# Set-up work of a fused four-layer kernel placed in other steps: bias scaling, decay, layer norm, w2 products and the adaptive layer

## The chip, the cores and the metric

The kernel runs on one core of a Trainium2 chip. A core has a matrix engine (TensorE, "PE" in the profile), a vector engine (VectorE, "DVE"), an activation engine (ScalarE, "ACT"), a general engine (GpSimd, "POOL") and an engine that only issues transfers (SyncE, "SP"). Each works through its own list of instructions in order and waits on semaphores for the others. Transfers are issued from SP, ACT or POOL. The metric is the time of the launch on the device in microseconds (us), the median of several runs.

## The reference

The input x has shape (4, 1024, 512): 4 sequences, 1024 time steps, width 512. Beside it there is one condition vector per sequence, cond (4, 512). Four layers are applied, each added to its own input:

```
x = x + rnn(x, h0=cond)           # h_t = tanh(x_t Wx0 + b0 + h_{t-1} Wh0)
x = x + ssm(x, conv_w=cond)       # conv of 4 taps, softplus, scan s_t = decay*s_{t-1} + dt*b_t*u_t, Wo
x = x + lstm(x, h0=cond)          # gates from x_t Wx2 + b2 + h_{t-1} Wh2
x = x + (x @ layer)               # layer = base + einsum(x_a, x_b), per sequence
    ae = layernorm(cond) * ln_g + ln_b
    x_a, x_b = split(gelu(ae @ w1 + b1) @ w2 + b2)    # w2 is (512, 2*512*8): 16.8 MB in float32
```

Two things are serial in time: the RNN and the LSTM, 1024 steps each. What depends on cond and weights alone (decay, folded convolution weights, the pieces of Wh2, the matrices `layer`) is worked out once.

## The kernel before, in words

Time is cut into 32 chunks of `TC` = 32 steps. `do_pass(c)` is one pass of 32 steps: in each step it does one LSTM step of chunk c, one RNN step of chunk c + 2, and spreads over the steps the projections for the RNN of chunk c + 3, the SSM layer of chunk c + 1, the LSTM's input products of chunk c + 1, and the adaptive layer of chunk c - 1. There are two passes ahead: pass -2 runs the RNN of chunk 0 alone, pass -1 the RNN of chunk 1 and the SSM of chunk 0. Pass 0 is the first with an LSTM.

Nothing is scheduled by a planner: the order on each engine is the order in which the Python code emits it (`manual_schedule`). Within step t of a pass this is: LSTM matmuls (L360), the jobs of place "pe" for this t, RNN matmuls (L335), the LSTM's vector and activation work with the jobs of place "gap", the RNN's transpose, add and tanh (L343, L344, L347), then what the dictionary `early` holds for (c, t), then the jobs of place "end". `early` carries the set-up work; `at(c, t, f)` adds to it.

The pieces of set-up that matter here, with their places before:

- `prepare_decay` (L243): 17 small VectorE instructions and one Exp, emitted ahead of pass -2.
- `scale_b2` (L263), step (-2, 0): scales the LSTM's bias. b2 arrives by 16 small transfers on the POOL queue.
- `split_wh2`, steps (-2, 4) to (-2, 29): cuts the 16 pieces of Wh2 in the tile `layer` into three bfloat16 parts each, on ScalarE and VectorE.
- `fold_conv` (L250), step (-2, 30): folds cond into the convolution weights.
- `load_late`, step (-2, 30): issues w1, the first four tiles of w2 and base on SP; they go to the parts of `layer` that the splitting has freed.
- `adapt_norm` and `adapt_hidden`, step (-1, 0): layer norm of cond, two sums over the width by matmuls with a matrix of 1/512 (L529, L540), Sqrt, then the product with w1 (L561) and Gelu.
- `adapt_w2(j)`, j = 0 to 31: one product of the hidden vector with a tile of w2 (16 matmuls of 64 columns, L578), four copies out of PSUM (L583), and the load of tile j + 4. The first 16 stand in every other step of pass -1, the other 16 in steps 0 to 15 of pass 0. After each half, `adapt_gather` moves the pieces by 16 small transfers on POOL.
- `adapt_bias`, `adapt_sum` (0, 19), `base_identity` (0, 0): transposes of b2's part, sums, and twice the identity added to base (16 VectorE instructions, L626).
- `adapt_layer(b, k)`, 16 of them, steps (0, 20) to (0, 31), four of these steps with two: a matmul of depth 8 over 512 columns (L617) and an addition that writes `layer` (L618).

All small results pass through two PSUM banks of tag "fill".

## Time and profile before

| | us |
|---|---|
| median of 3 runs | 4838.51 (4836.14 to 4839.81) |
| the profiled execution | 4832.98 |
| its span, first to last instruction | 4831.2 |
| first RNN matmul / second / third | 21.38 / 24.97 / 40.45 |
| first RNN matmul of pass -1 | 123.31 |
| first LSTM matmul of pass 0 / of pass 1 | 207.60 / 386.71 |

| engine | busy us | share of the span |
|---|---|---|
| TensorE | 4612.2 | 95% |
| VectorE | 3830.2 | 79% |
| ScalarE | 1734.0 | 36% |
| GpSimd | 50.2 | 1% |

The page shows one profiled execution. "L335" is a line of the code. In a timeline each line gives the start in us, the length, the engine, the line, the operation, output and input tiles with shapes, and in brackets how long the engine sat idle before it and what released it. A table by stretch gives for each stretch its length, the busy time of PE, PEld (TensorE's weight loads), DVE, ACT and POOL with the number of instructions, the clock that TensorE was granted (1.00 is full speed), the share of the DMA engines' time, and GB/s.

### The profile page before, as it was taken

The page shows a single profiled execution, that of the slowest core. Times are in us where ns is not written, and L with a number is a line of the kernel's source. Part 1 is how long each engine was busy: PE and PEld are TensorE (multiplying, and loading weights), DVE is VectorE, ACT ScalarE, POOL GpSimd, SP SyncE. Part 2 cuts the span into 40 slices and gives each one's busy share as a digit, 9 for nine tenths or more (in the row PEclk, how much of TensorE's full clock was granted, in tenths as well). Part 3 has the DMA queues.
Part 4 walks back from the last instruction along what each step waited for, and adds up shares of the span by engine and source line. Part 5 has one row for each costly group of instructions (what it writes and reads, how often), then busy time and mean ns, then how long its engine had stood idle before and what let it go on. Part 6 is the DMA issues. An engine that isn't in the chain of part 4 may idle for free.

```text
span 4831.2 us, 321596 instructions
## 1 busy us (share of the span) xinstructions
PE 4612.2 (95%) x147040; PEld 3528.0 (73%) x147040; DVE 3830.2 (79%) x17908; ACT 1734.0 (36%) x8647; POOL 50.2 (1%) x94
## 2 busy tenths in 40 slices
PE   5899999999999999999999999999999999999876
PEld 3677777777777777777777777777777777777654
DVE  3588887888888888888888888888888888888776
ACT  2233333333333333333333333333333333333332
POOL 2000000000000000000000000000000000000000
PEclk6999999999999999999999999999999999999999
DMA  6310000000000000000000000000000000000000
GB/s 135 100 35 9 9 9 7 7 9 9 9 9 7 9 7 9 9 9 9 7 7 9 9 9 9 7 9 7 9 9 9 7 9 7 9 7 7 6 3 7
DMA packets 38786, 67.46 MB, mean 14 GB/s; under 512 B 9056, under 2 KB 26080, under 8 KB 36400
## 3 DMA queue, kind: packets, MB, share of 16 engines
q1 hardware_dynamic: 33488, 45.63, 3.6%
q8 instruction: 1149, 18.83, 1.6%
q10 hardware_dynamic: 1728, 1.06, 0.1%
q14 instruction: 213, 1.74, 0.1%
q0 software_dynamic: 2208, 0.19, 0.1%
HBM read 38.34 MB, written 8.39 MB: 10 GB/s over the span
## 4 chain that ended last, share of the span: by engine, by line
PE 93%; DVE 5%; DMA 1%; issue 1%; ACT 0%; POOL 0%; DVEq 0%; SPq 0%; POOLq 0%
PE acc L360 58%; PE acc L335 18%; PE proj L316 9%; PE pb L290 3%; PE proj L290 2%; PE ada L674 2%; DVE tt L377 1%; DVE gc L382 1%; DVE h L187 1%; PE ssm_out L290 1%; DVE prod L393 0%; DVE h L406 0%; DVE gc L398 0%; DMA b<-in_b_dram 0%; PE pl L617 0%
## 5 line engine op out<-in xcount | busy, mean ns | idle before, releaser
L360 PE MATMUL acc<-wh,h 128*12 128x256 bf16 x98304 | 2875.3, 273 | 133.7 <-DVE h L187 130.4
L360 PEld LDWEIGHTS <-h 128*12 128x12 bf16 x98304 | 2266.3, 87 | 690.1 <-DVE h L187 367.3
L377 DVE STREAM_TRANSPOSE tt<-acc 128x256 f32<-128x256 f32 x2048 | 920.4, 449 | 419.9 <-PE acc L360 302.7
L335 PEld LDWEIGHTS acc<-wh,h 128*4 128x4 f32 x32768 | 813.0, 88 | 546.1 <-issue 208.6
L335 PE MATMUL acc<-wh,h 128*4 128x128 f32 x32768 | 1108.2, 276 | 49.5 <-ACT h L347 47.1
L389 ACT ACTIVATE gc<-gc 128x32 f32<-128x32 f32 x2048 | 469.7, 229 | 1053.2 <-DVE gc L382 963.1
L382 DVE TENSOR_REDUCE gc<-tt 128x32 f32<-128x128 f32 x2048 | 777.7, 380 | 35.3
L187 DVE TENSOR_TENSOR h<-h 128x8 f32<-128x8 f32 (+1 forms) x4098 | 680.3, 166 | 104.7
L403 ACT ACTIVATE th<-gc 128x8 f32<-128x8 f32 x2048 | 427.4, 209 | 829.3 <-DVE gc L398 829.3
L347 ACT ACTIVATE h<-pre 128x16 f32<-128x16 f32 x1024 | 221.4, 216 | 1166.8 <-DVE pre L344 1166.8
L316 PE MATMUL proj<-wx,x 128*32 128x512 f32 x4096 | 528.4, 592 | 1.3 <-DVE x L492 1.3
L406 DVE SCALAR_TENSOR_TENSOR h<-gc,th 128x8 f32<-128x8 f32 x2048 | 342.7, 167 | 221.6 <-ACT th L403 204.8
L398 DVE SCALAR_TENSOR_TENSOR gc<-prod 128x8 f32<-128x8 f32 x2048 | 342.0, 167 | 35.5
L343 DVE STREAM_TRANSPOSE tt<-acc 128x128 f32<-128x128 f32 x1024 | 316.0, 309 | 62.2 <-PE acc L335 62.1
L366 ACT COPY tt<-xw 128x32 f32<-128x32 f32 x2048 | 327.8, 207 | 0.0
L393 DVE SCALAR_TENSOR_TENSOR prod<-gc 128x16 f32<-128x16 f32 x2048 | 315.0, 154 | 0.0
L328 ACT ACTIVATE xw<-xw,b2s 128x64 f32<-128x64 f32 x1024 | 293.5, 334 | 0.4
L344 DVE TENSOR_TENSOR pre<-xw,tt 128x16 f32<-128x16 f32 x1024 | 179.5, 175 | 37.7 <-DVE tt L343 0.5
L290 PE MATMUL proj<-xin,wx 128*32 128x128 f32 x4096 | 138.9, 278 | 16.6 <-DMA wx<-in_Wx_dram 15.4
L290 PE MATMUL pb<-x,wp 128*32 128x128 f32 x4096 | 138.0, 274 | 0.8 <-issue 0.7
L674 PE MATMUL ada<-layer,x 128*32 128x512 f32 x1024 | 131.5, 592 | 3.0 <-DVE x L667 3.0
L290 PEld LDWEIGHTS proj<-xin,wx 128*32 128x32 f32 x4096 | 117.0, 112 | 19.9 <-issue 16.6
(114 smaller groups left out, 1172.9 us busy)
## 6 DMA issues: line engine op xcount, KB each, us to landing
layer<-in_w2T_dram SPq DMA_DIRECT2D x32, 512.0 KB, 3.6
xin<-in_xT_dram SPq DMA_DIRECT2D x128, 64.0 KB, 2.2
out_dram<-x SPq DMA_DIRECT2D x128, 64.0 KB, 1.7
layer<-in_Wh_dram SPq DMA_DIRECT2D x16, 256.0 KB, 9.6
wx<-in_Wx_dram SPq DMA_DIRECT2D x4, 1024.0 KB, 15.0
wx<-in_Wx_dram SPq DMA_DIRECT2D x4, 256.0 KB, 5.5
wh<-in_Wh_dram ACTq DMA_DIRECT2D x4, 256.0 KB, 6.5
layer<-in_w_dram SPq DMA_DIRECT2D x4, 256.0 KB, 4.3
```

The costliest lines, as they stand in the source:

```text
L187: nc.vector.tensor_tensor(h[:, :, n], h[:, :, n - 1], upper(h[:, :, n - 1]), ALU.subtract)
L290: nc.tensor.matmul(dst[CT * j : CT * (j + 1)], columns(j), x, start=first, stop=final)
L316: nc.tensor.matmul(ps[CT * j : CT * (j + 1), :], tok, w[:, j], start=(k == 0), stop=(k == KC - 1))
L335: nc.tensor.matmul(acc0[CT * j : CT * j + B, :], h[:, k, (t - 1) % TC, :], wh0[:, k, j * P : (j + 1) * P], start=(k == 0), stop=(k == KC - 1),
L360: nc.tensor.matmul(acc2[mh][CT * j : CT * j + NP * B, :], parts, w[:, :, n0 : n0 + 2 * CT], start=(k == 0 and n == 0), stop=(k == KC - 1 a ...
L366: nc.scalar.copy(tt2[m][t % 2][:, :, :, :B], xw2[c % 2][:, :, 2 * m : 2 * m + 2, t, :])
L377: nc.vector.transpose(self.tt[:, :, :, B:].rearrange("p g c b -> p (g c) b"), acc2[self.m])
L382: nc.vector.tensor_reduce(self.gc[:, :4].rearrange("p g c b -> p (g c) b"), self.tt[:, :, :, : (1 + NP) * B].rearrange("p g c (s b) -> p ( ...
L389: nc.scalar.activation(self.gc[:, :4], self.gc[:, :4], AF.Tanh)
L398: nc.vector.scalar_tensor_tensor(self.c, self.prod[:, 1], 0.5, self.prod[:, 0], ALU.mult, ALU.add)
L403: nc.scalar.activation(self.th, self.c, AF.Tanh, scale=0.5)
L406: nc.vector.scalar_tensor_tensor(self.out[:, :, 0], self.gc[:, 2], 1.0, self.th, ALU.add, ALU.mult)
```

## The change

The load of Wh0 is issued from SP after that of Wx0, no longer from ACT. `prepare_decay` goes to step (-2, 9), `scale_b2` to (-2, 12), `fold_conv` to (-2, 24). The layer norm is cut in two, `adapt_center` at (-2, 26) and `adapt_norm` at (-2, 28); the matrix of 1/512 is now written by GpSimd into a part of `xw2[0]`. `adapt_hidden` goes to (-1, 2), `base_identity` to (-1, 20), `adapt_bias` to (-1, 0) and (-1, 1). The 32 products of w2 stand in consecutive steps from (-1, 3) to (0, 2), and two of the four copies of each are ScalarE's. `adapt_sum` goes to (0, 7), `adapt_layer` to steps 8 to 30 of pass 0, at most one per step. In passes without an LSTM the RNN's projections stand in steps 8, 10, 12, 14 instead of 0, 10, 11, 12. Jobs of place "end" come ahead of those of `early`.

```diff
-    wh0 = load_rows(const, "wh0", a["Wh0"], D, nc.scalar)
+    wh0 = load_rows(const, "wh0", a["Wh0"], D, nc.sync)
...
-    def adapt_norm():
-
+    ae, xc, sq = (prep.tile([P, KC, B], F32, name=x, tag=x) for x in ("ae", "xc", "sq"))
+    ones = xw2[0][:, 0, 0].rearrange("p t b -> p (t b)")
+    nc.gpsimd.memset(ones, 1.0 / D)
+
+    def mean_over_width(x):
+        ps = bank("pp", [P, B])
+        for k in range(KC):
+            nc.tensor.matmul(ps, ones, x[:, k, :], start=(k == 0), stop=(k == KC - 1))
+        return ps
+
+    def adapt_center():
+        mean = prep.tile([P, B], F32, name="mean", tag="mean")
+        nc.vector.tensor_copy(mean, mean_over_width(condT))
+        nc.vector.tensor_tensor(xc, condT, mean.unsqueeze(1).to_broadcast([P, KC, B]), ALU.subtract)
+        nc.vector.tensor_mul(sq, xc, xc)
         nc.vector.tensor_copy(
             xab[:, :, :, :RANK],
             bm2.rearrange("p h k r -> p (h k) r").unsqueeze(2).to_broadcast([P, 2 * KC, B, RANK]),
         )
-        ones = xw2[1][:, 2, 0].rearrange("p t b -> p (t b)")
-        nc.vector.memset(ones, 1.0 / D)
...
+    def adapt_norm():
+
         rstd = prep.tile([P, B], F32, name="rstd", tag="rstd")
-        nc.vector.tensor_scalar(rstd, ps[:, 0, :], EPS, None, ALU.add)
+        nc.vector.tensor_scalar(rstd, mean_over_width(sq), EPS, None, ALU.add)
...
     def adapt_hidden():
 
-        ae = adapt_norm()
...
         for t in range(4):
-            nc.vector.tensor_copy(xr[CT * t : CT * t + B, half, hd, rg], ps[CT * t : CT * t + B, :])
+            copy = (nc.vector.tensor_copy, nc.scalar.copy)[t % 2]
+            copy(xr[CT * t : CT * t + B, half, hd, rg], ps[CT * t : CT * t + B, :])
...
-    early = {(-2, 0): [scale_b2], (-2, 30): [fold_conv], (-1, 0): [adapt_hidden], (0, 0): [base_identity]}
+    early = {
+        (-2, 9): [prepare_decay], (-2, 12): [scale_b2], (-2, 24): [fold_conv], (-2, 26): [adapt_center], (-2, 28): [adapt_norm],
+        (-1, 2): [adapt_hidden], (-1, 20): [base_identity],
+    }
...
+    for half in range(2):
+        at(-1, half, lambda half=half: adapt_bias(half))
+        at(0, 7, lambda half=half: adapt_sum(half))
     for j in range(NW2):
-        half = j // (NW2 // 2)
-        c, t = (-1, 2 * j + 1) if half == 0 else (0, j - NW2 // 2)
-        at(c, t, lambda j=j: adapt_w2(j))
+        c, t = divmod(3 + j, TC)
+        at(c - 1, t, lambda j=j: adapt_w2(j))
         if j % (NW2 // 2) == NW2 // 2 - 1:
-            at(c, t, lambda half=half: adapt_gather(half))
-    for half in range(2):
-        at(-1, 2 + 2 * half, lambda half=half: adapt_bias(half))
-        at(0, 19, lambda half=half: adapt_sum(half))
-    for b in range(B):
-        for k in range(KC):
-            at(0, 20 + (b * KC + k) * 3 // 4, lambda b=b, k=k: adapt_layer(b, k))
+            at(c - 1, t, lambda half=j // (NW2 // 2): adapt_gather(half))
+    for n in range(B * KC):
+        at(0, 8 + 3 * n // 2, lambda n=n: adapt_layer(n // KC, n % KC))
...
-                jobs += [((0, 10, 11, 12)[m], "pe", mm), ((0, 10, 11, 12)[m], "end", end)]
+                t = ((0, 10, 11, 12) if lstm else (8, 10, 12, 14))[m]
+                jobs += [(t, "pe", mm), (t, "end", end)]
...
+            do(t, "end")
             for f in early.pop((c, t), ()) if dst is None else ():
                 f()
-            do(t, "end")
...
-    prepare_decay()
     do_pass(-2, lstm=False, ssm=False, late=False)
```

More of the change, by code (lines that the diff above doesn't have):

```diff
@@ L524, in adapt_norm @@
         )
-        ones = xw2[1][:, 2, 0].rearrange("p t b -> p (t b)")
-        nc.vector.memset(ones, 1.0 / D)
-        ps = bank("pp", [P, KC, B])
-        for k in range(KC):
-            nc.tensor.matmul(ps[:, 0, :], ones, condT[:, k, :], start=(k == 0), stop=(k == KC - 1))
-        mean = prep.tile([P, B], F32, name="mean", tag="mean")
-        nc.vector.tensor_copy(mean, ps[:, 0, :])
-        xc = prep.tile([P, KC, B], F32, name="xc", tag="xc")
-        nc.vector.tensor_tensor(
-            xc, condT, mean.unsqueeze(1).to_broadcast([P, KC, B]), ALU.subtract
-        )
-        sq = prep.tile([P, KC, B], F32, name="sq", tag="sq")
-        nc.vector.tensor_mul(sq, xc, xc)
-        ps = bank("pp", [P, KC, B])
-        for k in range(KC):
-            nc.tensor.matmul(ps[:, 0, :], ones, sq[:, k, :], start=(k == 0), stop=(k == KC - 1))
+    def adapt_norm():
         rstd = prep.tile([P, B], F32, name="rstd", tag="rstd")
-        nc.vector.tensor_scalar(rstd, ps[:, 0, :], EPS, None, ALU.add)
+        nc.vector.tensor_scalar(rstd, mean_over_width(sq), EPS, None, ALU.add)
         nc.scalar.activation(rstd, rstd, AF.Sqrt)
         nc.vector.reciprocal(rstd, rstd)
-        ae = prep.tile([P, KC, B], F32, name="ae", tag="ae")
         nc.vector.tensor_mul(ae, xc, rstd.unsqueeze(1).to_broadcast([P, KC, B]))
@@ L550, in adapt_norm @@
             )
-        return ae
     def adapt_hidden():
-        ae = adapt_norm()
         ps = bank("pp", [P, P])
@@ L646, in cond_resid_kernel @@
     at(-2, 30, load_late)
+    for half in range(2):
+        at(-1, half, lambda half=half: adapt_bias(half))
+        at(0, 7, lambda half=half: adapt_sum(half))
     for j in range(NW2):
-        half = j // (NW2 // 2)
-        c, t = (-1, 2 * j + 1) if half == 0 else (0, j - NW2 // 2)
-        at(c, t, lambda j=j: adapt_w2(j))
+        c, t = divmod(3 + j, TC)
+        at(c - 1, t, lambda j=j: adapt_w2(j))
         if j % (NW2 // 2) == NW2 // 2 - 1:
-            at(c, t, lambda half=half: adapt_gather(half))
-    for half in range(2):
-        at(-1, 2 + 2 * half, lambda half=half: adapt_bias(half))
-        at(0, 19, lambda half=half: adapt_sum(half))
-    for b in range(B):
-        for k in range(KC):
-            at(0, 20 + (b * KC + k) * 3 // 4, lambda b=b, k=k: adapt_layer(b, k))
+            at(c - 1, t, lambda half=j // (NW2 // 2): adapt_gather(half))
+    for n in range(B * KC):
+        at(0, 8 + 3 * n // 2, lambda n=n: adapt_layer(n // KC, n % KC))
     def adapt_jobs(c, dst):
```

## The prediction

> **What bounds the kernel now.** I read the chain of work that ended last, then the busy times by stretch, then the order of instructions in the first 390 us, where all touched code runs. The page says TensorE carries the chain; its list of DMA issues prices a w2 tile:

> ```profile
> PE 93%; DVE 5%; DMA 1%; issue 1%; ACT 0%; POOL 0%; DVEq 0%; SPq 0%; POOLq 0%
> ...
> layer<-in_w2T_dram SPq DMA_DIRECT2D x32, 512.0 KB, 3.6
> ```

> By stretch (us, then busy us of each engine, granted clock, DMA share, GB/s):

> ```profile
> 77.00:123.00 46.00, 33.11 (x548) 19.33 (x552) 19.34 (x51) 12.48 (x34) 2.34 (x4) 0.50 0.21 59
> ...
> 172.00:208.00 36.00, 34.27 (x976) 21.79 (x972) 17.49 (x74) 7.27 (x32) 1.78 (x3) 1.00 0.37 121
> ...
> 240.00:300.00 60.00, 54.73 (x1990) 47.42 (x1982) 53.35 (x254) 19.15 (x97) 4.68 (x9) 1.00 0.23 72
> ...
> 2000.00:2143.00 143.00, 141.44 (x4572) 108.61 (x4564) 117.46 (x553) 53.47 (x269) 0.00 (x0) 1.00 0.03 8
> ```

> The last line is the steady state: one pass of 32 steps takes 142.6 us, 4.46 per step, TensorE full; no edit reaches it. Pass 0 runs from the first LSTM matmul at 207.60 to that of pass 1 at 386.71, 179.1 us, 36.5 over a steady pass. Passes -2 and -1 are a serial chain (matmul, transpose, add, tanh), at half clock in most of pass -2.

> The start, in order of time:

> ```profile
> 24.16 0.30 DVE L343 STREAM_TRANSPOSE tt<-acc 128x128 f32<-128x128 f32 x1
> ...
> 24.97 1.42 PE L335 MATMUL acc<-wh,h 128*4 128x128 f32 x32 [2.53 <-ACT h L347]
> ...
> 36.44 0.17 DVE L264 TENSOR_SCALAR b2s<-b 128x12 f32<-128x12 f32 x1 [11.78 <-DMA b<-in_b_dram]
> ...
> 39.52 0.17 DVE L265 COPY b2s<-b 128x4 f32<-128x4 f32 x1 [2.91 <-DMA b<-in_b_dram]
> 39.63 0.32 DVE L343 STREAM_TRANSPOSE tt<-acc 128x128 f32<-128x128 f32 x1
> ```

> Step 1 of the RNN ended on TensorE at 26.4; VectorE turned it at 39.63, because the scaling of b2, queued ahead, waited for 16 small transfers of the POOL queue.

> The head of pass -1, where the layer norm and hidden layer stand between two RNN steps:

> ```profile
> 123.31 1.63 PE L335 MATMUL acc<-wh,h 128*4 128x128 f32 x32
> ...
> 131.34 1.89 PE L561 MATMUL pp<-layer,ae 128*4 128x128 f32 x32 [2.00 <-DVE pp L557]
> ...
> 134.71 1.07 PE L335 MATMUL acc<-wh,h 128*4 128x128 f32 x32
> ```

> 11.4 us from step 0 to step 1. Later in that pass a product of w2 costs TensorE 0.45 us (186.15 to 186.60), an input projection 0.86, an RNN step 0.87:

> ```profile
> 186.15 0.63 PE L578 MATMUL pp<-layer,hid 128*4 128x64 f32 x32
> 186.60 1.04 PE L316 MATMUL proj<-wx,x 128*32 128x512 f32 x8
> 187.46 1.06 PE L335 MATMUL acc<-wh,h 128*4 128x128 f32 x32
> ```

> [...] 32 RNN matmuls last 1.89 us at clock 0.50 and 1.06 at 1.00; the clock rose after back-to-back work at 60 to 63 us and fell after 76.8, when they filled about 40% of a step. [...] 200 GB/s at share 1.0 from 24 to 40 us[...].

> **The change, part by part.** The sum stands against the profiled execution (4832.98; span 4831.2), which is 5.5 us under the median of the runs.

> *Wh0 behind wx0, decay and b2 out of the start.* Now wx0 (1 MB) shares the DMA engines with wh0 (1 MB), both landing near 16, and the projections start at 15.4. With wx0 first, 0.3 MB of xin and 1 MB at about 200 GB/s would be in by about 11 (its fourth issue still waits for condT, near 8, plus some 3 us). One projection of chunk 1, 0.87 us, also leaves this place: four take about 4.9, so they end at 16. Wh0's four SP issues (0.4 us each) follow at 8 to 10; 1 MB more lands at about 15.5 to 16, in time. RNN step 0 starts at 16 instead of 21.38. Its transpose no longer waits for the decay chain (it ended at 24.23; acc was ready at 22.44), so step 1 starts at 18.2 instead of 24.97 and is turned at about 19.7 instead of 39.63: **-19.9 us**. Bounds -15 (wx0 no earlier) to -21. What was behind the wh0 issues on SP (xin, Wh2, Wp, Ws, Wo, Wx2) moves the same bytes: layer[1] is 3.9 MB into the queue, in by about 24; the first split needs it at 27.

> *Pass -2.* The moved work lands in steps of 2.79 us in which VectorE is busy 0.5, or some 2 where Wh2 is split. b2 at step 12 (0.34) is hidden: step 12 splits nothing, and b2 is there at 40, the step at about 47; with its cover gone it would cost 0.34. The decay at step 9 is 17 small VectorE instructions around an Exp, some 3.2 us (21.0 to 24.2 for all but the first; its vec was there at 10.4), where some 2.2 are free: +1.3. adapt_center (step 26): four more matmuls at half clock, 1.7 in a gap of 0.9, and VectorE with the split ends at 4.0 instead of 2.8: +1.2. adapt_norm (step 28): table load, Sqrt, and a load back for the tanh (one load more than before), with seven VectorE instructions of 1.4: next tanh after 3.7 instead of 2.8: +0.9. fold_conv only moves; the ones, now a memset of POOL (0.22, as ident's), stand ahead of the wp scaling, which is early. Chunk 2's first projection leaves the head of pass -1 (-0.9); chunk 1's go to 8, 10, 12, 14, one more than steps 10 to 12 had, but keep the clock up there: -0.4 net with the decay left out. Sum **+2.1**; bounds -12 (clock full throughout: 15 steps less 0.8) to +7 (never full).

> *Pass -1.* Without the norm, steps 0 to 5 take 4.0 + 2.35 + 3.7 (hidden layer at step 2, waiting for its memset) + 2.3 + 3.3 = 15.7 instead of 21.5: -5.8. Steps 5 to 15 carry a product each instead of every other: +0.45 on TensorE in steps bound by a chain through VectorE, where half of the copies (4 of 0.22) now go to ScalarE at about 0.22 (nearest row: COPY 128x32, 0.21); with a slow-clock patch at 155 to 158 gone: -1. Steps 15 to 31 become TensorE-bound, 0.87 + 0.86 + 0.45 = 2.18 against 2.11: +1.2. base_identity at step 20, 16 instructions of 0.18 = 3.1, leaves 1.7 uncovered. Sum **-3.9**, bounds -8 to +3. The POOL gathers (16 of 0.57) start after steps 18 and (0, 2), five LSTM steps before adapt_sum needs them: hidden.

> The w2 loads now come one per step: 0.5 MB per 2.2 us, 240 GB/s, up to four ahead. In the 5 us from 175 they ran at 139 GB/s for a share of 0.45, so some 300 is available; even at the 205 of the start (2.56 us each) 28 loads take 72 + 3.5 us, and steps (-1, 3) to (0, 2) give them about 80. Hidden.

> *Pass 0.* 16 products go to 3, base_identity (3.1 of VectorE and, after its stall, an LSTM step at half clock, 4.40 instead of 2.79) leaves. Steps 0 to 2: TensorE 2.62 + 0.87 + 0.87 + 0.45, about 4.9 each; 3 to 5, 10, 13 and six later ones without a layer 4.46; 6 the same. Step 7 is VectorE: 3.47 bare (from a 5.25 us step with 0.92 of copies and 0.85 of ssm), turns and products 0.91, both adapt_sums 1.4: 5.75. Layers: at 8 and 9 VectorE 3.47 + 0.85 + 0.68 = 5.0, at 14 4.9, at the 13 other steps 4.46 + 1.05 (324.40 to 325.45) = 5.51. Total 160.4 against 179.1: **-18.8**, bounds -13 to -22.

> Sum: -19.9 + 2.1 - 3.9 - 18.8 = -40.5. Median 4838.51 - 40.5 = 4798.

> **Rivals.** *A, the loads hold pass -1 up in part:* each w2 load takes 3.2 us at full rate, through contention with xin and instruction fetch (TensorE's "issue" gaps, 3.4 us in pass 0, stand beside w2 loads). 28 x 3.2 + 3.5 - 80 = +13: 4811. Against it: landing times of 3.4 to 4.4 already hold the fixed part. A wx0 that lands no earlier (+5) goes with it. *B, a warm clock through pass -2:* the run of projection and RNN work at 11 to 17 us keeps it up; -14 more, 4784. Against: it fell after 76.8. *C, slower:* the w2 loads do not overlap, each landing before the next moves, in pass -1. The gain is gone at (80 + 40.5 - 3.5) / 28 = 4.2 us each, and it is 0.2% slower from 4.5; at 5 us: 140 + 3.5 - 80 - 40.5 = +23, 4862. Against: layer tiles of 256 KB with landing times of 9.6 us ran four and more at once at 200 GB/s. *D, nothing gained at the start,* another late transfer taking b2's place (layer[1], xin): -20.6, 4818. Against: the byte count above.

> **Numbers.** 0.2% (9.7 us) is about what can be told from no change. Forecast 0.68 (own range 4788 to 4808), A 0.14, B 0.08, D 0.05, C 0.05 (half of it slower, the rest within 0.2%). 4785 to 4813 leaves out C, D and part of B. Faster 0.94, same 0.03, slower 0.03.

> **What would show it.** RNN step 1 turned near 20 us, no wait on b2; first LSTM matmul near 186; pass 0 at about 160; no wait of the w2 products on their DMA. Wrong if the w2 products wait for transfers, if step 0 starts after 18, or if pass 0 stays over 170.

## The result and the profile after

The changed kernel takes 4810.77 us (median of six runs, 4806.80 to 4815.68), the kernel before 4836.15 in the same comparison (six runs, 4834.85 to 4839.81): a ratio of 0.9946, 95% interval 0.9933 to 0.9959. It is faster by 25.4 us, where 40.5 were forecast. The median lies outside the forecast's own range of 4788 to 4808, and inside the wider one of 4785 to 4813, which takes in rival A and part of B. The two profiled executions stand 26.2 us apart (4832.98 and 4806.80); the marks of this section are read from these two. That of the changed kernel is the fastest of its six runs.

The page's chain of work that ended last, and its row for the loads of w2:

```profile
PE 94%; DVE 5%; issue 1%; ACT 0%; DMA 0%; ACTq 0%; DVEq 0%; SPq 0%
...
layer<-in_w2T_dram SPq DMA_DIRECT2D x32, 512.0 KB, 4.1
```

TensorE still carries the chain. A w2 tile lands in 4.1 us instead of 3.6, below the 4.2 at which, by the forecast's rival C, the gain would be gone.

By stretch, with the columns of the table of the kernel before:

```profile
60.00:106.00 46.00, 35.20 (x536) 21.31 (x536) 20.48 (x59) 14.83 (x35) 2.35 (x4) 0.50 0.46 114
155.00:191.00 36.00, 33.43 (x1108) 24.34 (x1112) 18.04 (x84) 13.18 (x62) 8.46 (x15) 1.00 0.68 218
212.00:272.00 60.00, 56.98 (x1757) 44.07 (x1753) 50.55 (x232) 21.44 (x107) 3.72 (x7) 1.00 0.02 5
2000.00:2143.00 143.00, 141.34 (x4560) 108.53 (x4560) 117.18 (x551) 53.43 (x269) 0.00 (x0) 1.00 0.03 8
```

The last line, the steady state, is as in the kernel before. In the second, the end of pass -1, the loads now move 218 GB/s instead of 121, and TensorE has 1108 matmuls in 36 us instead of 976.

The start, from the timeline:

```profile
17.47 1.06 PE L335 MATMUL acc<-wh,h 128*4 128x128 f32 x32
...
18.60 0.32 DVE L343 STREAM_TRANSPOSE tt<-acc 128x128 f32<-128x128 f32 x1 [8.56 <-PE acc L335]
...
19.50 1.06 PE L335 MATMUL acc<-wh,h 128*4 128x128 f32 x32 [0.96 <-ACT h L347]
...
20.62 0.32 DVE L343 STREAM_TRANSPOSE tt<-acc 128x128 f32<-128x128 f32 x1 [1.43 <-PE acc L335]
```

Step 1 of the RNN is turned as soon as its matmuls end, at 20.62 instead of 39.63.

| first matmul of | before | after | gain in all | gain of this part |
|---|---|---|---|---|
| RNN step 2 | 40.45 | 21.45 | 19.0 | 19.0 |
| pass -1 | 123.31 | 107.02 | 16.3 | -2.7 |
| pass 0 (LSTM) | 207.60 | 190.53 | 17.1 | +0.8 |
| pass 1 (LSTM) | 382.25 | 353.43 | 28.8 | +11.75 |
| end of the span | 4831.2 | 4805.0 | 26.2 | -2.6 |

A correction belongs here. The text on record gives 386.71 as the first LSTM matmul of pass 1 of the kernel before. It is that of its second step; the first is at 382.25. Pass 0 of before took 174.65 us, not 179.1.

Where the rest went is seen on TensorE: it stops in the middle of its work, with nothing that the profile names as a releaser ("issue"). The list of waits of TensorE from 130 to 190 us, after (engine, tile and line, releaser: us in total, times, longest):

```profile
PE pp L575 <- issue: 2.7, 3, 1.2
PE proj L316 <- issue: 1.5, 1, 1.5
PE proj L316 <- DVE layer L581: 1.1, 1, 1.1
...
PE acc L335 <- issue: 0.7, 1, 0.7
```

In the kernel before, the same stretch has no such entry. No product of w2 (L575) waits for a transfer. One such stop lies in pass -2 too, inside step 14 of the RNN, after 28 of its 32 matmuls:

```profile
52.98 1.04 PE L335 MATMUL acc<-wh,h 128*4 128x128 f32 x28
55.89 0.39 PE L335 MATMUL acc<-wh,h 128*4 128x128 f32 x4 [1.86 <-issue]
```

I call these stops gaps. Until 430 us they sum to 9.1 us in the changed kernel and to 4.7 in the kernel before.

### The profile page after: what moved, and what is told of

It reads as the page before. It is cut to its first block, busy times and chain, and to the rows that moved or that the text cites. A ratio compares the mean times of both kernels' runs of the same rounds, so it can differ in the third digit from the quotient of the medians.

```text
span 4805.0 us, 321617 instructions
## 1 busy us (share of the span) xinstructions
PE 4609.9 (96%) x147040; PEld 3529.9 (73%) x147040; DVE 3816.7 (79%) x17843; ACT 1749.1 (36%) x8712; POOL 52.1 (1%) x95
## 3 DMA queue, kind: packets, MB, share of 16 engines
q8 instruction: 1149, 18.83, 1.7%
## 4 chain that ended last, share of the span: by engine, by line
PE 94%; DVE 5%; issue 1%; ACT 0%; DMA 0%; ACTq 0%; DVEq 0%; SPq 0%
PE acc L360 58%; PE acc L335 18%; PE proj L316 9%; PE pb L290 3%; PE proj L290 2%; PE ada L673 2%; DVE tt L377 1%; DVE gc L382 1%; DVE h L187 1%; PE ssm_out L290 1%; DVE h L406 1%; DVE prod L393 0%; DVE gc L398 0%; PE pl L615 0%; PE pp L575 0%
## 5 line engine op out<-in xcount | busy, mean ns | idle before, releaser
L335 PEld LDWEIGHTS acc<-wh,h 128*4 128x4 f32 x32768 | 815.6, 88 | 521.3 <-issue 212.2
L335 PE MATMUL acc<-wh,h 128*4 128x128 f32 x32768 | 1109.1, 276 | 31.6 <-ACT h L347 27.8
L347 ACT ACTIVATE h<-pre 128x16 f32<-128x16 f32 x1024 | 221.4, 216 | 1144.7 <-DVE pre L344 1144.7
L316 PE MATMUL proj<-wx,x 128*32 128x512 f32 x4096 | 529.5, 592 | 2.6 <-issue 1.5
L343 DVE STREAM_TRANSPOSE tt<-acc 128x128 f32<-128x128 f32 x1024 | 316.2, 309 | 70.3 <-PE acc L335 70.1
L290 PE MATMUL proj<-xin,wx 128*32 128x128 f32 x4096 | 138.8, 278 | 11.9 <-DMA wx<-in_Wx_dram 11.8
L290 PEld LDWEIGHTS proj<-xin,wx 128*32 128x32 f32 x4096 | 117.1, 112 | 14.0 <-DMA wh<-in_Wh_dram 11.8
## 6 DMA issues: line engine op xcount, KB each, us to landing
layer<-in_w2T_dram SPq DMA_DIRECT2D x32, 512.0 KB, 4.1
wx<-in_Wx_dram SPq DMA_DIRECT2D x4, 1024.0 KB, 15.5
```

The source lines that it names most:

```text
L290: nc.tensor.matmul(dst[CT * j : CT * (j + 1)], columns(j), x, start=first, stop=final)
L316: nc.tensor.matmul(ps[CT * j : CT * (j + 1), :], tok, w[:, j], start=(k == 0), stop=(k == KC - 1))
L335: nc.tensor.matmul(acc0[CT * j : CT * j + B, :], h[:, k, (t - 1) % TC, :], wh0[:, k, j * P : (j + 1) * P], start=(k == 0), stop=(k == KC - 1),
```

## The experiments

My theory after this reading: the start gained what was forecast, and what is missing comes from the miscounted step and from the gaps, in which TensorE's instructions arrive late beside bulk transfers. Rivals: the gaps come from how dense the instructions stand, whatever the transfers do; the start is due to one of its two edits alone; the clock of pass -2.

For all runs I compare the start of the RNN's tanh in step 31 of a pass, since each tanh is in the trace one by one. A column "pass" is the time from one such mark to the next, in us of the profiled execution; "pass -2" is counted from the tanh of step 2. Each ratio is to runs of the kernel before in the same comparison.

| kernel | median us | ratio to before, 95% | tanh of step 2 | pass -2 | pass -1 | pass 0 | pass 1 |
|---|---|---|---|---|---|---|---|
| before | 4836.15 | | 43.04 | 79.4 | 85.6 | 175.4 | 143.0 |
| after | 4810.77 | 0.9946 (0.9933 to 0.9959) | 23.20 | 83.6 | 84.2 | 163.8 | 144.7 |
| b2 alone | 4830.71 | 0.9988 (0.9982 to 0.9995) | 32.00 | 85.3 | 85.3 | 175.1 | 142.9 |
| Wh0 back on ScalarE | 4815.96 | 0.9956 (0.9944 to 0.9969) | 26.48 | 83.1 | 85.0 | 163.9 | 145.0 |
| w2 and layer in old places | 4808.60 | 0.9945 (0.9933 to 0.9958) | 22.76 | 86.7 | 76.3 | 174.0 | 143.8 |
| four w2 loads | 4803.94 | 0.9939 (0.9926 to 0.9953) | 23.34 | 84.3 | 80.7 | 166.0 | 142.8 |
| old places, four w2 loads | 4805.22 | 0.9933 (0.9920 to 0.9947) | 22.93 | 80.9 | 76.8 | 171.9 | 143.2 |
| Wx2 held back | 4800.12 | 0.9932 (0.9920 to 0.9945) | 22.59 | 80.3 | 84.2 | 164.0 | 143.9 |
| b2 alone, Wx2 held back | 4819.61 | 0.9974 (0.9963 to 0.9984) | 32.54 | 79.8 | 84.0 | 175.1 | 143.4 |
| fill of eight | 4817.81 | 0.9967 (0.9954 to 0.9979) | 24.50 | 94.4 | 83.5 | 165.2 | 143.3 |
| fill of eight, Wx2 held back | 4813.66 | 0.9956 (0.9944 to 0.9969) | 24.75 | 91.3 | 83.2 | 165.5 | 143.9 |
| fill of three | 4798.45 | 0.9928 (0.9915 to 0.9940) | 22.29 | 78.1 | 82.0 | 163.1 | 143.4 |
| fill of three, Wx2 held back | 4800.83 | 0.9935 (0.9923 to 0.9947) | 22.77 | 79.4 | 83.4 | 163.7 | 143.6 |
| the same, w2 in five of six steps | 4807.02 | 0.9946 (0.9933 to 0.9960) | 23.01 | 80.9 | 80.4 | 171.4 | 143.0 |

One caution for reading it: five kernels (after, Wh0 back, old places, four loads, old places with four loads) have the same instructions in pass -2, and their profiles give 80.9 to 86.7 us for it. A difference in pass -2 below some 5 us between two single profiles shows nothing. Passes -1 and 0 repeat far better: after and Wh0 back, which are the same there, give 84.2 and 85.0, 163.8 and 163.9.

### b2 alone

The kernel before, with one edit:

```diff
-    early = {(-2, 0): [scale_b2], (-2, 30): [fold_conv],
+    early = {(-2, 12): [scale_b2], (-2, 30): [fold_conv],
```

> The kernel before with one edit, the scaling of b2 at step (-2, 12) in place of (-2, 0). By the sum: the turn of RNN step 1 comes right behind its matmuls, near 26.8 us instead of 39.63, so -12.9 us; the first pieces of Wh2 were issued from 16.6 us with a landing time of 9.6, so step 4 finds them. The profiled run should give about 4820, ratio 0.9973. By rival D (another late transfer takes the place of b2): a wait of 5 to 13 us on a piece of Wh2 or on xin shows up at steps 1 to 6, and the time stays at 4828 to 4833.

Measured: 5.0 us by the medians of this comparison (4835.73 to 4830.71), not 12.9; the profiled run took 4830.43 and not 4820. The wait on b2 is gone, and no other transfer takes its place, so rival D falls, although the time is the one that it gave. From the timeline of TensorE:

```profile
25.85 1.06 PE L335 MATMUL acc<-wh,h 128*4 128x128 f32 x29 [2.53 <-ACT h L347]
27.96 0.59 PE L335 MATMUL acc<-wh,h 128*4 128x128 f32 x3 [1.05 <-issue]
...
58.71 0.28 PE L335 MATMUL acc<-wh,h 128*4 128x128 f32 x2 [2.37 <-issue]
...
67.92 0.59 PE L335 MATMUL acc<-wh,h 128*4 128x128 f32 x3 [1.60 <-issue]
```

By the tanh of step 2, 11.0 us are gained: 12.9, less 0.87 by which step 0 came later in this execution (22.25 instead of 21.38), less the first gap of 1.05. Pass -2 then took 85.3 instead of 79.4: 4.0 of these 5.9 us are the other two gaps; the 1.9 left lie within what single profiles differ by. So the wait was worth 12.9 where it stood and less than half of it at the end.

### Wh0 back on ScalarE

```diff
-    wh0 = load_rows(const, "wh0", a["Wh0"], D, nc.sync)
+    wh0 = load_rows(const, "wh0", a["Wh0"], D, nc.scalar)
```

> The changed kernel with the load of Wh0 back on ScalarE's queue. If the order of wx0 and wh0 is what starts the RNN earlier: both share the transfer engines again, wx0 lands near 15.4 instead of 11.8, the four projections (5.85 us) end near 20.5 to 21, RNN step 0 starts there instead of 17.47, and the whole is +3 to +3.5 us (0.07%, seen in the marks of the profile, hardly in the medians). If the queue does not matter, or SP's issues were the limit: step 0 within 0.5 us of 17.47.

The timeline of TensorE in this run:

```profile
15.15 5.79 PE L290 MATMUL proj<-xin,wx 128*32 128x128 f32 x128 [15.15 <-DMA wx<-in_Wx_dram]
20.75 1.06 PE L335 MATMUL acc<-wh,h 128*4 128x128 f32 x32
```

Wx0 is there at 15.15 instead of 11.81, and step 0 starts at 20.75 instead of 17.47: 3.3 us, as expected. In the nine other runs with the changed start it came at 16.5 to 17.8, so the delay is more than single profiles differ by. The medians (4815.96 against 4810.77) point the same way, but their ratios overlap.

### w2 products and layer in their old places

```diff
-        (-1, 2): [adapt_hidden], (-1, 20): [base_identity],
+        (-1, 2): [adapt_hidden], (0, 0): [base_identity],
...
-        at(0, 7, lambda half=half: adapt_sum(half))
+        at(0, 19, lambda half=half: adapt_sum(half))
...
-        c, t = divmod(3 + j, TC)
+        c, t = (0, max(3 + j, 2 * j + 1)) if j < 16 else (1, j - 16)
...
-        at(0, 8 + 3 * n // 2, lambda n=n: adapt_layer(n // KC, n % KC))
+        at(0, 20 + n * 3 // 4, lambda n=n: adapt_layer(n // KC, n % KC))
```

> The changed kernel with the w2 products (every other step of pass -1, then steps 0 to 15 of pass 0), their gathers, the sums (0, 19), the layer matmuls (0, 20 to 31) and the identity (0, 0) in the places that they had before. Start, passes -2 and the head of pass -1 stay as changed. If moving them is worth what the marks of the two kernels say: pass 0 goes from 162.9 back to about 174.5, pass -1 from 83.5 to about 79 (13 products fewer at 0.45, 1.7 of the identity, and no gaps of instruction supply), pass 1 gives back 2.6: about +5 us, 4812 profiled against 4806.8. If the move is worth the 18.8 of the prediction less the miscounted step (14.3), and the gaps of pass -1 are not due to the doubled rate of loads: +10 to +12.

Pass 0 goes back to 174.0, 10.1 us longer, and pass -1 falls to 76.3, 7.9 shorter. With 0.9 more in pass 1 of the changed kernel, 1.3 us are left of the largest part of the change, and the medians cannot be told apart (4808.60 and 4810.77), against both expectations. TensorE's waits from 130 to 190 us here, whole:

```profile
PE acc L335 <- ACT h L347: 4.9, 4, 2.1
PE ssm_out L290 <- DVE w L480: 1.4, 1, 1.4
PE proj L316 <- DVE x L492: 1.3, 1, 1.3
```

With a product in every other step, pass -1 has no gap. Twelve gaps, 7.5 us in all, stand in pass 0 instead, where the second half of the products is.

### Four w2 loads, with the products as changed

```diff
         if j + W2_BUFS < NW2:
-            load_w2(j + W2_BUFS)
+            w2[j + W2_BUFS] = w2[j]
```

> The changed kernel with only the first four of the 32 w2 tiles loaded; every product reads one of these four again, so the layer matrices are computed from wrong weights; instructions of TensorE, VectorE and ScalarE are the same ones. If TensorE's gaps for which the profile finds no releaser (4.8 us in pass -1, 1.5 in pass 0, 0.7 in pass 1) come from instruction fetches held up by the loads: those of passes -1 and 0 go, -5 to -7 us. If they come from the density of the instructions themselves: they stay in place, and the time is within 2 us.

Pass -1 takes 80.7 instead of 84.2 (85.0 in the run with Wh0 moved back), and one gap is left from 130 to 190 us:

```profile
PE acc L335 <- issue: 0.5, 1, 0.5
```

So in pass -1 most of the gaps need the loads: 3.5 us come back, where the theory gave 5 to 7 for both passes. In pass 0 they don't need them: 2.5 us of gaps stand in its first four steps, as in the changed kernel, with 18 GB/s moving on average (188 to 209 us). Pass 0 is 2.2 us longer here, and a patch at a granted clock of 0.76 from 235 to 242 us is part of it. On the whole the gain over the changed kernel is not separated from none (0.9939 against 0.9946).

### Four w2 loads, with the products in their old places

The same edit in the kernel with the old places, the third experiment.

> The kernel of the third experiment (w2 products every other step of pass -1 and in steps 0 to 15 of pass 0, as in the kernel before), with only the first four of the 32 w2 tiles loaded, so that the layer matrices come from wrong weights; the instructions of TensorE are the same. In the third experiment pass 0 had twelve gaps without a releaser in steps 2 to 18, 7.5 us together, and took 173.2 us. If they are instruction fetches held up by the loads of w2 (110 GB/s there): at most 2 are left, in the first steps, where they also stood without loads in the fourth experiment, and pass 0 takes about 168. If they come from the number of instructions in those steps (five groups of TensorE per step): 6 to 8 stay, and pass 0 takes 172 or more.

TensorE's waits from 185 to 275 us, first in the old places with all loads, then without the 28:

```profile
PE pp L575 <- issue: 4.0, 5, 1.3
PE acc L360 <- issue: 2.0, 3, 0.8
```

```profile
PE acc L360 <- issue: 2.6, 5, 0.7
...
PE pp L575 <- issue: 0.6, 2, 0.3
```

All entries of this kind together go from 7.5 to 4.5 us, and pass 0 from 174.0 to 171.9. Neither expectation holds alone. Where an LSTM step, an RNN step, a projection and a product share a step, more than half of the gaps stay with 28 of 32 loads away; the loads make them longer. Pass 0 of the kernel before has gaps of the same kind (4.7 us). Pass -1 has next to none at this spacing, with the loads or without (76.3 and 76.8 us).

### Wx2 held back

```diff
-    wx2 = load_rows(const, "wx2", a["Wx2"], 4 * D, nc.sync)
+    wx2 = const.tile([P, KC, 4 * D], F32, name="wx2", tag="wx2")
+    def load_wx2():
+        nc.vector.memset(wx2[:, 0, 0:1], 0.0)
+        quads(nc.sync, wx2, a["Wx2"].rearrange("(j c q) n -> j q c n", j=4, c=KC))
...
+    at(-2, 16, load_wx2)
```

On SP, w1 and the first four w2 tiles are issued behind Wx2 (in the changed kernel Wx2 from 43.26 us, w1 from 45.66, w2 from 51.08), so they are held back with it: 32 GB/s move from 40 to 60 us in this run, 185 in the changed kernel.

> The changed kernel with the load of Wx2 (4 MB) held back to step (-2, 16), about 62 us, by one small memset of its tile; it is first read in step 15 of pass -1. In all four kernels seen in which the RNN starts early, TensorE stops in the middle of a group of RNN matmuls between 55 and 60 us, for 1.5 to 2.4 us, with no releaser, while Wx2 fills the transfer engines; the kernel before has no such gap. If the instruction fetch waits behind bulk transfers: no gap near 56, pass -1 starts 1.5 to 2 us sooner than 107.0 (at 105), or the gap is met again in the 20 us behind the new place of the load. If the fetch is late for its own reasons: the gap stays at the same matmul, between 55 and 60.

There was no gap near 56 us, one of 1.1 at 38 while Wh2 was loaded, and none from 60 to 100, where 208 GB/s moved and then 209. Pass -2 took 80.3, but by the caution above that is no proof, and the ratio (0.9932) overlaps that of the changed kernel. "In all four kernels" in the expectation did not last either: the run of the old places with four loads has none at 55 to 60.

The same edit on top of b2 alone:

> The kernel before with the scaling of b2 at step (-2, 12), as in the first experiment, and Wx2 held back to (-2, 16). The first experiment gained 12.5 us by RNN step 2 and had 5.1 left at pass -1, with three gaps without a releaser, 1.05 at 28, 2.37 at 58.7 and 1.60 at 67.9. If the fetch waits behind bulk transfers, the last two go and pass -1 starts near 114 in place of 118.2, the whole 4 us below the first experiment. If not, they stay and nothing is gained.

"12.5 us by RNN step 2" in it is a misreading of the first experiment; it is 11.0. Here the effect is all but separated: 4819.61 us, 0.9974 (0.9963 to 0.9984) against 0.9988 (0.9982 to 0.9995), two intervals that overlap by 0.0002. That is 12.8 us under before instead of 5.0. That it equals the price of b2's wait is in part chance: by the profile 1.6 us of it were gained in pass -1 (84.0 instead of 85.6), and no run holds Wx2 back in the kernel before alone. TensorE's waits from 20 to 107 us, whole (L340 here is L335 of the others):

```profile
PE acc L340 <- ACT h L352: 27.9, 27, 2.5
PE proj L295 <- ACT xw L309: 0.2, 1, 0.2
```

No gap at all, where b2 alone had 5.0 us. The gap at 28 us went too, although Wh2 was being loaded as before, so part of this difference is chance as well.

### Fill matmuls in pass -2

```diff
                 rnn_mm(c + 2, t)
+            if c == -2:
+                for k in range(8):
+                    nc.tensor.matmul(acc2[0][:B, :P], condT[:, k % KC, :], wh0[:, k % KC, :P], start=True, stop=True)
```

> The changed kernel with eight matmuls of 128 columns added behind the RNN's in every step of pass -2, into rows of a PSUM tile that the first LSTM step overwrites; nothing reads their result. If the half clock of pass -2 comes from TensorE being idle for more than half of a step, the fill (0.95 us at half clock, beside 1.89 of a 2.79 us step) keeps the full clock: steps that split Wh2 take 2.5, the others 2.0, the three with set-up 3.4 to 4.05, so pass -2 ends 10 to 12 us sooner, near 96, and the whole is 4795 to 4800. If the fill is fetched too late (its instructions double TensorE's in that pass, while bulk loads run): gaps without a releaser grow from 2 to 5 us or more and eat half of it. If the clock does not follow: 0 to +2.

The clock followed (0.98 from 20 to 118 us), and the time did not. From 80 to 100 us (columns as above):

```profile
80.00:100.00 20.00, 20.00 (x367) 16.64 (x357) 9.57 (x25) 5.67 (x15) 1.33 (x3) 1.00 0.16 54
```

TensorE is full, at clock 1.00, because I had mis-sized the fill. Each of its eight matmuls is two pieces in the trace; in a step of 2.62 us, 1.06 are the RNN's, which leaves 97 ns for each of the fill's 16 pieces where I had taken 33. Beside that the gaps grew to 9.2 us, 3.2 the longest. With Wx2 held back as well, 4813.66 us; the gaps of pass -2 were one of 0.9, one of 2.2 and one of 1.6:

> The two edits of the runs before it together: Wx2 held back and fill matmuls in pass -2. If both effects stand on their own: pass -1 starts near 94, 12 to 14 us sooner than in the changed kernel, 4793 to 4797. If the gaps only move to the new place of the load: as with the fill alone.

With `range(3)`:

> The changed kernel with three fill matmuls per step in pass -2 in place of the eight of the run with the fill. There each of the 16 pieces of a fill held TensorE for 97 ns at full clock [...], 1.55 us per step, so every step took 2.62 and the clock gained nothing. Six pieces are 0.58, less than the 0.94 us that a step leaves idle. If the half clock of pass -2 is due to idleness: the clock stays at 1.00, steps of 2.0 and 2.5, pass -1 starts 8 to 12 us sooner than 107.0, less the gaps without a releaser (1.5 to 3 us more of them than in the changed kernel, since bulk loads run), the whole 4798 to 4803. If one in three steps is still too idle (a split step has 1.64 of 2.5 busy): the clock falls, steps of 3.06 at half clock, and nothing is gained.

TensorE's waits from 20 to 107 us (L749 is the fill), then the granted clock (the column ahead of the last two) in two stretches:

```profile
PE acc L335 <- ACT h L347: 13.4, 24, 1.6
PE acc L749 <- issue: 4.1, 1, 4.1
PE acc L335 <- issue: 3.2, 3, 1.9
```

```profile
17.00:55.00 38.00, 28.64 (x690) 22.07 (x678) 18.36 (x62) 10.84 (x32) 19.81 (x35) 1.00 0.96 198
61.00:67.00 6.00, 6.00 (x80) 3.75 (x78) 2.28 (x6) 1.26 (x3) 0.00 (x0) 0.57 1.01 208
```

The clock stays up until 59.3, inside a gap of 4.13 us that ends at 60.6, and is back at 66.1. Pass -2 takes 78.1, of which 7.3 are gaps: 70.8 without them, against 81.5 in the changed kernel without its 2.1. That is 10.7 us, within the 8 to 12 at which the clock was priced, and half of it (5.2) went to more gaps. This version has the lowest median, 4798.45 (4795.02 to 4801.47); its slowest run is faster than the fastest of the changed kernel, but the ratios still overlap (0.9928 with 0.9915 to 0.9940, against 0.9946 with 0.9933 to 0.9959).

> Three fill matmuls per step and Wx2 held back to step (-2, 16). If both effects stand on their own (3.9 us of the held-back load by pass -1's start, 8 to 11 of the clock): pass -1 starts at 92 to 96, 4788 to 4793, ratio near 0.991. If the gaps only move: 4797 to 4800, as with Wx2 held back alone.

4800.83 us: the two effects don't add. The gaps of pass -2 were 6.1 us in four pieces, in other places.

> As the run before it, with the w2 products in five of six steps from (-1, 3) to (0, 8), the sums at (0, 13), the layer matmuls in steps 14 to 29 of pass 0. If the gaps of pass -1 come from the rate of loads: the 4 to 5 us of gaps of pass -1 fall to 2 to 3 at 200 GB/s in place of 217, five products move from pass -1 to pass 0 at no net cost, 1 to 3 us gained. If the products cost the same wherever they stand: within 1.5 us of the run before it.

Edit: `divmod(3 + 6 * j // 5, TC)`, sums at (0, 13), layers at `(0, 14 + n)`. Pass -1 gained 3.0 and pass 0 lost 7.7, 4.8 of it in gaps (6.0 us instead of 1.2): 4807.02, against both expectations. Moving products from pass -1 to pass 0 was no free exchange.

## Why the prediction was right, and where it failed

By profiled executions the sum was -40.5 and the result -26.2. A misread mark (4.5) and the gaps (9.1), for which the sum had nothing, add up to 13.6 of the 14.3 between them; smaller misses stand beside them. Part by part:

- *Start, -19.9:* measured -19.0. Step 1 is turned at 20.62 (forecast 19.7). Wx0 came at 11.8 (11), and four projections took 5.85 (4.9). Parts: 3.3 for the queue of Wh0, by its own run; 12.9 for b2's wait, seen as 11.0 beside a later start and one gap. From RNN step 0 to step 1, where the decay stood, it is 2.0 us instead of 3.6. 0.9 missing.
- *Pass -2, +2.1:* measured +2.7, with two gaps (2.1 us) that the sum did not have. Decay's step took 4.05 (2.79 + 1.3), the centring 3.67 (4.0), the norm 3.62 (3.7), with two table loads of 1.28 us in it (97.79 and 99.31) and Sqrt between them, 0.02 us behind the first and 0.01 ahead of the second. In the five kernels with the same instructions here, pass -2 takes 80.9 to 86.7, and its gaps 1.0 to 2.4. 0.6 missing.
- *Pass -1, -3.9:* measured -0.8. The head was right: steps 0 to 5 take 15.9 in the old places (15.7 forecast, 21.5 before) and 16.8 here, where the clock is half for the first 4.8 us instead of 3.3. The count of TensorE's work was right too: with four loads nearly all of steps 15 to 31 take the 2.18 forecast, and the pass, from its first RNN matmul to the first of the LSTM, takes 80.0 us, 4.3 less than before. With all 32 loads it takes 83.5. The step that failed is the "Hidden" of the w2 loads. They are hidden from the products, none of which waits for its data; but with them TensorE loses 3.5 us in this pass that it does not lose with four loads, and the sum put that at nothing. 3.1 missing.
- *Pass 0, -18.8:* measured -11.75. 4.46 of the difference is the miscounted step of before, an error of reading alone: 160.4 against 174.65 is -14.25. Steps 0 to 2 take 5.65, 5.07 and 6.34 (4.9 each), 2.4 more, with gaps of 1.5 among them; steps 3 to 5 another 0.6. The rest is as worked out: 4.45 in steps without additions, 5.74 where the sums land (5.75), 5.51 for a layer step (5.51). 7.05 missing.
- *From pass 1 on, nothing:* measured +2.6, 1.85 of it in steps 2 to 6 of pass 1, with gaps of 0.2 to 0.3. Pass 1 is 142.8 to 145.0 in the runs above.

Of what was to show it, the turn near 20 us and the missing waits on b2 and on w2's transfers came; the first LSTM matmul came at 190.5 (186), pass 0 took 162.9 (160). None of the three signs of being wrong came. The terms that failed were the size of pass 0, by a misread mark, and the pricing by TensorE's busy time, as if its instructions were always there.

What the gaps are can be read from the traces. The page of the changed kernel:

```profile
PE 4609.9 (96%) x147040; PEld 3529.9 (73%) x147040; DVE 3816.7 (79%) x17843; ACT 1749.1 (36%) x8712; POOL 52.1 (1%) x95
...
q8 instruction: 1149, 18.83, 1.7%
```

The last line is of the table of DMA queues (transfers, MB, share of the 16 engines' span). The queue q8 carries instructions in 1149 transfers of 16 KB. Only TensorE has enough of them for that: 147040 matmuls and as many weight loads are 256 instructions for each transfer (all other instructions of the trace are 27537), so one block is 128 matmuls with their weight loads. The packed traces hold the start and length of every transfer. In the fourteen traces there are 167 gaps up to the end of pass 1. Counted in TensorE's instructions modulo 256, its waits on semaphores among them, they all stand at one place, give or take one (192 or 193 for the 14 of the changed kernel and the 8 of the kernel before); I take it for the border between two blocks. Each ends 1.0 to 1.7 us after a transfer of q8 has ended (median 1.4; 98% lie within 1.1 to 1.7, where 14% of moments drawn at random would; 1.2 to 1.6 in the two kernels compared). From this I read that in a gap TensorE waits for its next block of instructions. One stop of 1.1 us at 150.2, which the list of waits puts down to VectorE (L581), stands beside that place too (195, 1.5 us behind the end of a transfer).

The traces also give the times by which both loads and density come in. Paired by number, the transfer of a block starts about when TensorE crosses the border before that block: in the median 0.5 us later in the steady state and in pass -1 with four loads, 1.4 in pass -1 of the changed kernel, and up to 7.0 in its pass -2, while Wh2 and Wx2 are loaded. The transfer takes about 1.0 us (up to 1.5 in the changed kernel until 430 us), and TensorE can go on 1.4 us later. By these medians, which make this an estimate, a block that TensorE works off in less than 2.9 us (3.8 beside the w2 loads) ends in a gap. Blocks take 4.2 us in the steady state, 2.8 to 5.4 in pass -1, 3.2 to 3.7 in the opening of pass 0, where the transfers start 1.1 to 1.7 us behind the border, and 6 to 12 in pass -2. The same bulk loads cost the kernel before no gap in pass -2, since its blocks, with the wait on b2 and a slower clock, took 11 us or more while the transfers started latest (6.2 us behind the border; the clock is 0.50 from 25.5 to 63.1). No run changes the instruction transfers themselves.

Of the rivals, A gave 4811, from a rate of 3.2 us a load that I had assumed. That is the measured number, and half of its mechanism fits. Its transfers do not hold the products up: no product waits for one. The 3.5 us in pass -1 and 2.1 in pass 0 of the old places that the runs without loads gain fit its contention between w2 loads and instruction fetch. But the number fits by adding other terms, 13 for waits that did not occur; that it is hit is luck. B is excluded by the clock of 0.50 from 60 to 106, C by the absence of any wait on w2's transfers, D by the start.

How much idleness lets the clock fall is not shown. In the kernel before it fell to 0.50 at 76.7 us, and TensorE's longest idle stretch from 63 us to there is 1.46 us; in the changed kernel it fell at 29.9, behind stretches of at most 0.97 us.

What stays open: why the gaps of pass -2 differ between executions (1.0 to 2.4 us in the five kernels that have the same instructions there), why the instruction transfers start later in the opening of pass 0 than in the steady state when little else is moving, and why pass 1 has gaps in some kernels and not in others. No run isolates the moves of the decay, of the layer norm and of the identity, the copies given to ScalarE, or the new order of the places "end" and `early`.

## What to carry to other kernels

Price a moved instruction on TensorE at its busy time only where the profile of that stage shows no "issue" gaps (pass -1 here: -3.9 us by busy time, -0.8 measured). Where it does, count TensorE's instructions in blocks of one instruction transfer (here 128 matmuls with their weight loads) and compare the time of a block with the time that the next one needs to arrive, here about 2.9 us by the estimate above, and 3.8 beside the w2 loads. A move between two stages that are both at this limit can be a wash, as that of the w2 products and the layer was (1.3 us). Read the gain of a removed stall at the end of the set-up and not where the stall stood: b2's was worth 11.0 us there and 5.0 at the end, with 4.0 us of gaps beside bulk loads of 136 to 193 GB/s in between. Count the steps of a pass from one repeated instruction that the trace has one by one, before taking a pass's length from it.
